# Basis products of a relational graph convolution: ten edge groups per product, one basis after each of eight groups

## The chip, the cores and the metric

The kernel runs on one core of a Trainium2 chip. The time is the device time of one execution in microseconds (us). The engines work in parallel, each through its own queue of instructions, and wait for each other through semaphores: TensorE (PE in the profile, with PEld for its weight loads) multiplies matrices into PSUM, VectorE (DVE) and ScalarE (ACT) work on tiles, GpSimd (POOL) here issues the indirect DMAs that gather rows, and SyncE (SP) issues most other DMAs.

## What is computed

A graph of 30,000 nodes with 128 features and 960,000 edges sorted by destination goes through two layers. The first holds two relational convolutions, whose 32 relation matrices are mixtures of 8 bases; the second holds a gated convolution with 4 edge types.

```python
def _rel_graph_conv(h, basis, coeff, bias, src, dst, etype, norm):
    W = jnp.einsum('rb,bdf->rdf', coeff, basis)          # R = 32, B = 8, D = 128
    Hr = jnp.einsum('nd,rdf->nrf', h, W)
    msg = Hr[src, etype] * norm
    agg = jax.ops.segment_sum(msg, dst, num_segments=N)
    return agg + bias
h = jax.nn.relu(_rel_graph_conv(feat, basis1, coeff1, bias1, src, dst, etype, norm))
out = _rel_graph_conv(h, basis2, coeff2, bias2, src, dst, etype, norm)
...
for t in range(T):                                       # the gated layer, T = 4
    eta = jax.nn.sigmoid(k[dst] + q[src])
    msg = jnp.where((edge_type == t)[:, None], eta * v[src], 0.0)
    agg = jax.ops.segment_sum(msg, dst, num_segments=n)
```

## The kernel before

There are three passes over the edges: pass 1 ("c1", first relational convolution), pass 2 ("c2", second) and pass 3 ("g", the gates). The change touches the body of passes 1 and 2, `rel_body` (from L415).

**Tiling.** 128 edges make one gather, G = 3 gathers a group, S = 5 groups a block (index `s`), NS = 20 blocks or NG = 100 groups one iteration of the device loop, and NI = 25 iterations a pass. So a pass has 7,500 gathers, 2,500 groups and 500 blocks. Every five blocks (SB) are a stage with loads of its own indices.

**A group.** GpSimd gathers the source nodes' rows of three times 128 edges into `hg` (L118; five buffers, so five groups or 15 gathers may be on their way). Since the edges are sorted, a group's destinations lie in a window of W = 32 nodes. VectorE builds for each gather a row block `sb` (L515, 12 buffers): for each of the 8 bases, the edge's coefficient where the window's column is the edge's destination. TensorE multiplies rows by `sb` and accumulates the three products of 128x256 into `pa` (L520, three buffers), which holds 8 bases x 32 columns. ScalarE copies `pa` into the block's tile `ab` (L524, two buffers).

**A block.** The bases are applied after the sum over edges. `bases_out(s - 1)` (L476 to L482) runs after group 1 of block `s`: eight products in a row, one per basis, each with the basis as weights and 5 x 32 = 160 columns of `ab[s - 1]`, accumulated in `po` (L479). After group 3 of block `s`, `add_windows` (L410 to L413) adds the five windows of `po[s - 2]` into the node sums `agg`, which lie in SBUF, at columns that come from registers; a stage's registers are loaded at L400, after group 3 of its second block.

**The rest of a block.** In pass 1 the coefficients are made on the way: `types` loads relation numbers (SyncE, L436), `onehot` after group 3 compares them (VectorE, `oh`, L444) and multiplies with the coefficients (TensorE, four products into `cp`, L449), `coefficients` after group 2 scales them (VectorE, `ce`, L459), and `keep` stores those of the second convolution. Pass 2 reads these back (`kept`). The constant `iw` that `sb` is compared with lies in the PSUM bank of `cp`. `beside(n)` runs the steps on finished nodes (`after_first`, `after_second`) that are due after group `n`.

**Order.** The engines' orders are as the code is written (`manual_schedule`); the tile framework adds the waits for data and for free buffers. At the end of an iteration the last block's products and the last two blocks' additions follow at once. `late` in an assertion (L338 to L340) is the first group by which all sums of earlier windows must be added, before the nodes' steps read them.

Of the kernel before, what the change touches and what calls it, by code (L numbers as in the profile page):

```python
# [19 lines left out]
P = 128  # L20
# [8 lines left out]
B = 8  # L29
# [5 lines left out]
W = 32  # L35
# [37 lines left out]
def kernel(  # L73
# [261 lines left out]
    def sorted_path():  # L335

        for u in range(NPI // VB):
            late = min(g for g in range(NG)  # L338
                       if min((g // S + 2) * S + S - 2, NG) > u * PERIOD + 1)
            assert (u + 1) * VB - late * NPI // NG <= LEAD  # L340
        with ExitStack() as all_:
            def edge_pass(name, body, after, banks, extra=None):
# [67 lines left out]
            def add_windows(po, base, s):  # L410
                for g in range(S):
                    to = agg[:, ds(base[s % SB * S + g], W)]
                    nc.vector.tensor_add(to, to, po[:, g, :])  # L413

            def rel_body(table, weights, second):  # L415
# [5 lines left out]
                def body(bas, i, io, pool, ps, cp, iw, ic, beside):  # L421
                    stage = {}
                    er, oh, pc, ce, ce_next, ab, po, base = {}, {}, {}, {}, {}, {}, {}, {}

                    def loads(k):
                        stage[k] = [stage_tile(io, "idx", src, I32, i, k),
                                    stage_tile(io, "relc", reld, F32, i, k),
                                    firsts(io, i, k)]
                        if not second:
                            stage[k].append(  # L430
                                stage_tile(io, "nrm", norm, F32, i, k, 4 * TQ - S * G))

                    def types(s):
                        er[s] = pool.tile([P, TQ, TP], I32, name="er")
                        for c in range(TQ):
                            nc.sync.dma_start(  # L436
                                er[s][:, c, :],
                                bass.AP(tensor=et32_row.tensor,
                                        offset=(i * NG + s * S) * GE + c * TP,
                                        ap=[[TQ * TP, 4], [0, R], [1, TP]]))  # L440

                    def onehot(s):
                        oh[s] = pool.tile([P, TQ, TP], F32, name="oh")
                        nc.vector.tensor_scalar(oh[s], er[s], icol4, None, op0=ALU.is_equal)  # L444
                        at = TQ * 8 * B
                        pc[s] = cp[:TP, at:2 * at].rearrange("p (c q l b) -> p c q l b", c=TQ, q=4,
                                                             l=2)
                        for c in range(TQ):
                            nc.tensor.matmul(pc[s][:, c].rearrange("p q l b -> p (q l b)"),  # L449
                                             lhsT=oh[s][:, c, :],  # L450
                                             rhs=coeff.rearrange("p q l b -> p (q l b)"),
                                             start=True, stop=True)

                    def coefficients(s):
                        t0 = s % SB * S * G
                        nrm = stage[s // SB][-1][:, t0:t0 + 4 * TQ]
                        for to, l in ((ce, 0), (ce_next, 1)):
                            to[s] = pool.tile([TP, 4, TQ, B], F32, name=f"ce{l}")
                            nc.vector.tensor_mul(  # L459
                                to[s], pc[s][:, :, :, l].rearrange("p c q b -> p q c b"),  # L460
                                nrm.rearrange("p (q c) -> p q c", q=4).unsqueeze(3).to_broadcast(
                                    [TP, 4, TQ, B]))
                            to[s] = to[s].rearrange("p q c b -> p (q c) b")

                    def block_rows(s):
                        return ce2[ds(i * NS + s, 1)].rearrange("o p e -> (o p) e")

                    def keep(s):
                        nc.scalar.dma_start(block_rows(s), ce_next[s][:, :S * G, :].rearrange(
                            "p t b -> p (t b)"))  # L470

                    def kept(s):
                        ce[s] = pool.tile([TP, S * G, B], F32, name="ce", bufs=4)
                        nc.sync.dma_start(ce[s].rearrange("p t b -> p (t b)"), block_rows(s))

                    def bases_out(s):  # L476
                        po[s] = ps.tile([P, S, W], F32, name="po")
                        for b in range(B):
                            nc.tensor.matmul(po[s].rearrange("p s w -> p (s w)"),  # L479
                                             lhsT=bas[:, b, :],  # L480
                                             rhs=ab[s][:, b].rearrange("p s w -> p (s w)"),
                                             start=(b == 0), stop=(b == B - 1))  # L482

                    loads(0)
                    if second:
                        kept(0)
                        kept(1)
                    else:
                        types(0)
                        onehot(0)  # L490
                        coefficients(0)
                        types(1)
                        onehot(1)
                    for s in range(NS):
                        k = s // SB
                        if s % SB == 0:
                            if s:
                                tc.stage_boundary()
                            if k + 1 < NQ:
                                loads(k + 1)  # L500
                        if s % SB == 2:
                            leave_stage()
                        idx, relc, start = stage[k][:3]
                        if s + 2 < NS:
                            (kept if second else types)(s + 2)
                        ab[s] = pool.tile([P, B, S, W], F32, name="ab")
                        for g in range(S):
                            t0 = (s % SB * S + g) * G
                            hg = pool.tile([TP, G, D], F32, name="hg", bufs=5)
                            for j in range(G):  # L510
                                gather(hg[:, j, :], table, idx[:, t0 + j:t0 + j + 1])
                            pa = ps.tile([P, B, W], F32, name="pa", bufs=3)
                            for j in range(G):
                                sb = pool.tile([TP, B, W], F32, name="sb", bufs=12)
                                nc.vector.scalar_tensor_tensor(  # L515
                                    sb, iw[:TP].unsqueeze(1).to_broadcast([TP, B, W]),
                                    relc[:, t0 + j:t0 + j + 1],
                                    ce[s][:, g * G + j, :].unsqueeze(2).to_broadcast([TP, B, W]),
                                    op0=ALU.is_equal, op1=ALU.mult)
                                nc.tensor.matmul(pa.rearrange("p b w -> p (b w)"),  # L520
                                                 lhsT=hg[:, j, :],
                                                 rhs=sb.rearrange("p b w -> p (b w)"),
                                                 start=(j == 0), stop=(j == G - 1))
                            nc.scalar.copy(ab[s][:, :, g, :], pa)  # L524
                            if g == 1 and s:
                                bases_out(s - 1)
                            if g == 2 and not second and s + 1 < NS:
                                coefficients(s + 1)
                            if g == 3 and not second:
                                keep(s)  # L530
                                if s + 2 < NS:
                                    onehot(s + 2)
                            if g == 3 and s > 1:
                                add_windows(po[s - 2], base[(s - 2) // SB], s - 2)
                            if g == 3 and s % SB == 1:
                                base[k] = bases(start, DVE)
                            beside(s * S + g)
                    bases_out(NS - 1)
                    for s in (NS - 2, NS - 1):
                        add_windows(po[s], base[NQ - 1], s)  # L540
                return start

            def gate_body(i, io, pool, ps, cp, iw, ic, beside):
# [497 lines left out]
```

## Time and profile before

| | |
|---|---|
| median of 10 runs | 33,956.33 us (33,933.54 to 33,987.04) |
| the profiled execution | 33,942.56 us |
| its span, first to last instruction | 33,940.8 us |
| mean granted TensorE clock | 0.677 of full |
| busy: TensorE / weight loads | 59% / 50% |
| busy: GpSimd / VectorE / ScalarE | 63% / 37% / 11% |
| pass 1, first to last gather | 170.2 to 11,499.2 us |
| pass 2 | 11,531.1 to 22,412.9 us |
| pass 3 | 22,455.4 to 33,910.1 us |

A row of the profile's groups names the source line, the engine, the operation, the tiles (out<-in) and their shape, then the count, the busy time, the mean duration of one in ns, and how long the engine stood idle just before these instructions with the releaser that ended most of it. An fp32 product shows as two records of matmul and two of weight load, so 8,000 basis products of both passes are 16,000 records. A gather (L118) is the time GpSimd takes to issue it; its data land later. "remote" names a semaphore that came late although its sender had long been done; "issue" is time in which nothing awaited shows. The chain that ended last is empty for this execution.

### The profile page before, as it was taken

Reading aid. Unit: us, or ns where it says so; the run is one execution under the profiler, and the core shown is the slowest. Engines: PE = TensorE matmul, PEld = TensorE weight load, DVE = VectorE, ACT = ScalarE, POOL = GpSimd, SP = SyncE. Lnnn points to the kernel's source line nnn. Section 1 sums busy time; section 2 is a strip of 40 time slices with the busy share of each in tenths; the row PEclk is TensorE's granted clock in tenths of the full one; section 3 lists DMA queues with packets and bytes.
Section 4 is the critical chain, followed back from the end, with each engine's and each line's share of the span. In section 5 each row is a group of like instructions: output and inputs, shape, how many; then the busy total and the mean of one; then the engine's idle time right before and its main releaser. Section 6 shows DMA issues by size and latency. Waiting matters only on the chain.

```text
span 33940.8 us, 321543 instructions
## 1 busy us (share of the span) xinstructions
PE 19859.2 (59%) x83304; PEld 16928.3 (50%) x83304; DVE 12397.5 (37%) x32695; ACT 3634.6 (11%) x9834; POOL 21338.8 (63%) x22514
## 2 busy tenths in 40 slices
PE   4555555555555565666666666655555555555555
PEld 3444444444444444444444444445555555555555
DVE  4333333333333333333333333333333333333333
ACT  1000000000000011111111111111111111111111
POOL 5666666666666666666666666666666666666665
PEclk7777777777777777777777777765555555555555
DMA  3222222222222222222222222234444444444444
GB/s 101 64 64 63 64 64 65 64 64 64 65 62 63 65 66 66 66 66 67 66 66 66 67 66 66 66 100 124 124 124 124 124 124 125 125 124 124 124 124 120
DMA packets 2171202, 2914.97 MB, mean 86 GB/s; under 512 B 684764, under 2 KB 1617880, under 8 KB 2169544
## 3 DMA queue, kind: packets, MB, share of 16 engines
q0 software_dynamic: 840000, 1967.52, 21.7%
q1 hardware_dynamic: 923347, 651.19, 6.6%
q10 hardware_dynamic: 406197, 276.11, 2.8%
q8 instruction: 802, 13.14, 0.2%
q14 instruction: 856, 7.01, 0.1%
HBM read 2618.79 MB, written 274.16 MB: 85 GB/s over the span
## 4 chain that ended last, share of the span: by engine, by line


## 5 line engine op out<-in xcount | busy, mean ns | idle before, releaser
L118 POOL DMA_INDIRECT hg<-h,idx x15000 | 14207.2, 947 | 8177.9 <-issue 4280.9
L520 PE MATMUL pa<-sb,hg 128*128 128x256 f32 x30000 | 9137.1, 462 | 5956.2 <-issue 3770.4
L520 PEld LDWEIGHTS pa<-sb,hg 128*128 128x128 f32 x30000 | 6848.7, 237 | 7745.1 <-issue 4196.6
L118 POOL DMA_INDIRECT qv<-qvtab,qi x7500 | 7104.6, 947 | 4392.7 <-issue 2261.3
L515 DVE SCALAR_TENSOR_TENSOR sb<-cp,relc,ce 128x256 f32<-128x256 f32 x15000 | 6133.9, 475 | 5281.9 <-remote 4211.6
L588 PE MATMUL po<-sel,msg 128*128 128x32 f32 x15000 | 3462.9, 387 | 4601.5 <-DVE msg L586 3925.0
L588 PEld LDWEIGHTS po<-sel,msg 128*128 128x128 f32 x15000 | 3426.7, 328 | 4889.3 <-DVE msg L586 4092.3
L577 PE MATMUL pk<-kw,oh 128*128 128x128 f32 x15000 | 3974.7, 438 | 140.8 <-issue 96.1
L618 DVE TENSOR_TENSOR pk<-pk,qv 128x384 f32<-128x384 f32 x2500 | 1406.4, 563 | 7099.9 <-remote 5179.8
L524 ACT COPY ab<-pa 128x256 f32<-128x256 f32 x5000 | 1813.0, 373 | 19833.4 <-remote 9555.0
L577 PEld LDWEIGHTS pk<-kw,oh 128*128 128x128 f32 x15000 | 3468.0, 331 | 143.5 <-issue 143.5
L479 PE MATMUL po<-ab,bas 128*128 128x160 f32 x16000 | 2525.0, 314 | 463.9 <-issue 268.7
L479 PEld LDWEIGHTS po<-ab,bas 128*128 128x128 f32 x16000 | 2435.1, 202 | 589.1 <-issue 315.4
L413 DVE TENSOR_TENSOR agg<-agg,po 128x32 f32 x7500 | 1399.2, 187 | 2697.8 <-ACT xs L692 684.5
L619 ACT ACTIVATE pk<-pk 128x384 f32<-128x384 f32 x2500 | 1187.5, 475 | 9412.2 <-DVE pk L618 6201.7
L715 PE MATMUL bank<-wall,hT 128*120 128x512 f32 x1524 | 1047.3, 811 | 1020.7 <-ACT hT L711 369.7
L586 DVE TENSOR_TENSOR msg<-pk,qv 128x384 f32<-128x384 f32 x2500 | 1363.9, 546 | 0.0
L449 PE MATMUL cp<-coeff,oh 128*128 128x64 f32 x4000 | 670.9, 307 | 770.0 <-issue 599.4
L449 PEld LDWEIGHTS cp<-coeff,oh 128*128 128x128 f32 x4000 | 668.6, 231 | 851.9 <-issue 748.0
L564 DVE TENSOR_TENSOR oh<-kb,cp 128x1920 f32<-128x1920 bf16 x500 | 1071.4, 2143 | 47.6 <-issue 31.8
L726 DVE TENSOR_TENSOR kt<-bank,ball 120x512 f32<-120x512 f32 x254 | 175.7, 692 | 2338.1 <-PE bank L715 1044.2
L715 PEld LDWEIGHTS bank<-wall,hT 128*120 128x120 f32 x1524 | 351.6, 248 | 1353.9 <-issue 627.4
(77 smaller groups left out, 3382.7 us busy)
## 6 DMA issues: line engine op xcount, KB each, us to landing
hg<-h,idx POOLq DMA_INDIRECT x15000
kb<-kcode SPq DMA_DIRECT2D x500, 480.0 KB
kw<-ktab SPq DMA_DIRECT2D x2500, 64.0 KB
er<-in_et_row SPq DMA_DIRECT2D x2000, 64.0 KB
qvtab<-qvt ACTq DMA_DIRECT2D x254, 480.0 KB
qv<-qvtab,qi POOLq DMA_INDIRECT x7500
ktab<-kt ACTq DMA_DIRECT2D x254, 240.0 KB
ce<-ce ACTq DMA_DIRECT2D x500, 60.0 KB
```

The lines of the kernel that those rows point to most:

```text
L118: nc.gpsimd.indirect_dma_start(out=to, out_offset=None, in_=table, in_offset=bass.IndirectOffsetOnAxis(ap=idx, axis=0))
L413: nc.vector.tensor_add(to, to, po[:, g, :])
L449: nc.tensor.matmul(pc[s][:, c].rearrange("p q l b -> p (q l b)"), lhsT=oh[s][:, c, :], rhs=coeff.rearrange("p q l b -> p (q l b)"), start= ...
L479: nc.tensor.matmul(po[s].rearrange("p s w -> p (s w)"), lhsT=bas[:, b, :], rhs=ab[s][:, b].rearrange("p s w -> p (s w)"), start=(b == 0), ...
L515: nc.vector.scalar_tensor_tensor(sb, iw[:TP].unsqueeze(1).to_broadcast([TP, B, W]), relc[:, t0 + j:t0 + j + 1], ce[s][:, g * G + j, :].uns ...
L520: nc.tensor.matmul(pa.rearrange("p b w -> p (b w)"), lhsT=hg[:, j, :], rhs=sb.rearrange("p b w -> p (b w)"), start=(j == 0), stop=(j == G ...
L524: nc.scalar.copy(ab[s][:, :, g, :], pa)
L577: nc.tensor.matmul(pk[n][:, j, :], lhsT=oh[n // S][:, n % S, j * TP:(j + 1) * TP], rhs=kw[n], start=True, stop=True)
L586: nc.vector.tensor_mul(msg, pk[n], qv[n][:, :, 1, :])
L588: nc.tensor.matmul(po[s][:, g, :], lhsT=msg[:, j, :], rhs=sel[s][:, g * G + j, :], start=(j == 0), stop=(j == G - 1))
L618: nc.vector.tensor_add(pk[n], pk[n], qv[n][:, :, 0, :])
L715: nc.tensor.matmul(bank(a, VB, T * D), lhsT=hT, rhs=wall[:, a].rearrange("p t f -> p (t f)"), start=True, stop=True)
```

## The change

Blocks are taken in pairs, `q = s // 2`, with ten groups. `ab` becomes one tile per pair of twice the size, and so does `po`. In place of eight products of 160 columns after group 1 of each block, one product of 320 columns follows each of the group positions 1 to 8 of the next pair: basis 0 after position 1, basis 7 after position 8. The ten windows of a pair are added together after position 9. At an iteration's end the last pair's eight products of 320 columns and its ten additions follow at once. The assertion's `late` is adapted to the later additions.

```diff
@@ -336,7 +336,7 @@
             late = min(g for g in range(NG)
-                       if min((g // S + 2) * S + S - 2, NG) > u * PERIOD + 1)
+                       if min(g // (2 * S) * 2 * S + 2 * S + B + 1, NG) > u * PERIOD + 1)
@@ -473,13 +473,18 @@
-                    def bases_out(s):
-                        po[s] = ps.tile([P, S, W], F32, name="po")
-                        for b in range(B):
-                            nc.tensor.matmul(po[s].rearrange("p s w -> p (s w)"),
-                                             lhsT=bas[:, b, :],
-                                             rhs=ab[s][:, b].rearrange("p s w -> p (s w)"),
-                                             start=(b == 0), stop=(b == B - 1))
+                    def basis_out(q, b):
+
+                        if b == 0:
+                            po[q] = ps.tile([P, 2 * S, W], F32, name="po")
+                        nc.tensor.matmul(po[q].rearrange("p s w -> p (s w)"),
+                                         lhsT=bas[:, b, :],
+                                         rhs=ab[q][:, b].rearrange("p s w -> p (s w)"),
+                                         start=(b == 0), stop=(b == B - 1))
+
+                    def add_pair(q):
+                        for s in (2 * q, 2 * q + 1):
+                            add_windows(po[q][:, s % 2 * S:(s % 2 + 1) * S, :], base[s // SB], s)
@@ -503,7 +508,9 @@
-                        ab[s] = pool.tile([P, B, S, W], F32, name="ab")
+                        q = s // 2
+                        if s % 2 == 0:
+                            ab[q] = pool.tile([P, B, 2 * S, W], F32, name="ab")
@@ -521,23 +528,23 @@
-                            nc.scalar.copy(ab[s][:, :, g, :], pa)
-                            if g == 1 and s:
-                                bases_out(s - 1)
+                            nc.scalar.copy(ab[q][:, :, s % 2 * S + g, :], pa)
+                            if q and 0 < s % 2 * S + g <= B:
+                                basis_out(q - 1, s % 2 * S + g - 1)
...
-                            if g == 3 and s > 1:
-                                add_windows(po[s - 2], base[(s - 2) // SB], s - 2)
+                            if q and s % 2 * S + g == B + 1:
+                                add_pair(q - 1)
...
-                    bases_out(NS - 1)
-                    for s in (NS - 2, NS - 1):
-                        add_windows(po[s], base[NQ - 1], s)
+                    for b in range(B):
+                        basis_out(NS // 2 - 1, b)
+                    add_pair(NS // 2 - 1)
                 return start
```

## The prediction

> **What bounds the kernel now.** I read the groups of instructions first, then the waits, the idle and busy stretches of each engine, and the timeline around two gaps. GpSimd is the busiest engine (63%), so its groups come first, with those that the change touches.
>
> ```profile
> L118 POOL DMA_INDIRECT hg<-h,idx x15000 | 14207.2, 947 | 8177.9 <-issue 4280.9
> L520 PE MATMUL pa<-sb,hg 128*128 128x256 f32 x30000 | 9137.1, 462 | 5956.2 <-issue 3770.4
> ...
> L524 ACT COPY ab<-pa 128x256 f32<-128x256 f32 x5000 | 1813.0, 373 | 19833.4 <-remote 9555.0
> ...
> L479 PE MATMUL po<-ab,bas 128*128 128x160 f32 x16000 | 2525.0, 314 | 463.9 <-issue 268.7
> ...
> L413 DVE TENSOR_TENSOR agg<-agg,po 128x32 f32 x7500 | 1399.2, 187 | 2697.8 <-ACT xs L692 684.5
> ```
>
> A gather takes 0.947 us, and where nothing is awaited the next follows 0.30 us later: a pace of 1.25 us. 7,500 gathers at 1.251 us are 9,383 us per pass. By the starts of the first and last gather the three passes took 11,329 us (pass 1, first relational layer), 10,882 (pass 2, second layer) and 11,455 (pass 3, gates). Counting every start in the trace, the excess over 1.25 us sits in single gaps: 720 in pass 1 (1,945 us, 2.70 each) and 636 in pass 2 (1,499 us, 2.36 each). These gaps are all that a change beside the gathers can move. The waits name who ends them:
>
> ```profile
> ACT ab L524 <- remote: 9555.0, 1105, 17.9
> ...
> DVE sb L515 <- remote: 4211.6, 524, 20.3
> ...
> POOL hg L118 <- remote: 2209.2, 898, 4.8
> ...
> POOL hg L118 <- PE pa L520: 1213.3, 606, 14.5
> ```
>
> (waiter, releaser: us in total, times, longest.) "remote" is a release by an engine that had been done long before. The timeline of two blocks in pass 1 shows it (start, duration, engine, count, idle time before):
>
> ```profile
> 8010.66 2.75 PE L520 MATMUL pa<-sb,hg 128*128 128x256 f32 x12
> 8013.25 1.00 PE L449 MATMUL cp<-coeff,oh 128*128 128x64 f32 x8
> ...
> 8020.11 0.95 POOL L118 DMA_INDIRECT hg<-h,idx  x1 [0.30 <-issue]
> ...
> 8024.17 0.37 ACT L524 COPY ab<-pa 128x256 f32<-128x256 f32 x1 [14.94 <-remote]
> ...
> 8024.47 4.79 DVE L515 SCALAR_TENSOR_TENSOR sb<-cp,relc,ce 128x256 f32<-128x256 f32 x12 [11.81 <-remote]
> 8024.64 0.95 POOL L118 DMA_INDIRECT hg<-h,idx  x1 [3.59 <-remote]
> ...
> 8031.43 2.34 PE L479 MATMUL po<-ab,bas 128*128 128x160 f32 x16
> ...
> 8042.41 0.94 POOL L118 DMA_INDIRECT hg<-h,idx  x1 [0.30 <-issue]
> ...
> 8046.84 0.37 ACT L524 COPY ab<-pa 128x256 f32<-128x256 f32 x1 [14.84 <-remote]
> ...
> 8047.07 0.94 POOL L118 DMA_INDIRECT hg<-h,idx  x1 [3.72 <-remote]
> ...
> 8047.54 1.08 DVE L413 TENSOR_TENSOR agg<-agg,po 128x32 f32 x5 [16.31 <-ACT ab L524]
> ```
>
> TensorE ended at 8014.25, yet the copy and the selection rows that need its signals start only at 8024.2. GpSimd, whose five group buffers (15 gathers) are then used up, stops, and all three resume within 0.5 us. Read one by one, the semaphore events show why: while gathers run, TensorE's increments and SyncE's issues come 0.70 us apart, as if one path took them in turn. Once the gathers have stopped and landed, those held back come 0.04 us apart. By the trace's counts a block of five groups has 28.0 increments of TensorE and 22.0 issues of SyncE in pass 1, so 0.70 x 50 = 35.0 us against a mean block of 11,329/500 = 22.66 us. In pass 2 it is 26.0 + 8.5 = 34.5, 24.2 us against 21.76. Both are over the block's time, so signals fall behind until a gap lets them out.
>
> TensorE isn't the bound: it is idle some 40% of both passes. One stretch in each of passes 1 and 2 (busy time of TensorE, its loads, VectorE, ScalarE and GpSimd, then the granted clock, DMA share and GB/s):
>
> ```profile
> 5000.00:6000.00 1000.00, 569.53 (x2461) 480.57 (x2459) 351.98 (x1050) 90.23 (x267) 635.16 (x671) 0.75 0.25 64
> 15000.00:16000.00 1000.00, 612.05 (x2344) 462.28 (x2344) 374.53 (x1080) 106.38 (x320) 652.97 (x691) 0.78 0.26 66
> ```
>
> **The change, part by part.** *Products.* A pair of blocks had 2 x 8 products of 160 columns and gets 8 of 320. The columns stay (2,560), so streaming costs 0. Half of the loads go (8,000 of 202 ns, which overlap the products). Hidden by TensorE's idle 40%; if that cover were gone, their exposed part would be a gain. Each product increments once, so a block has 4 increments fewer: 24.0 in pass 1, 22.0 in pass 2.
>
> *Pass 2, signals.* 0.70 x (22.0 + 8.5) = 21.35 us per block, just below the 21.76 that a block takes now. I take it that signals then set the pace: 500 x (21.35 - 21.76) = -205 us. Lower end: stalls shrink with the lag that a stall-free block gathers. Such a block is 15 x 1.251 = 18.77 us and takes 26.8 signals. The lag goes from (34.5-26.8)/34.5 = 0.22 to (30.5-26.8)/30.5 = 0.12, 46% less: -685 us. Upper end: the adds' new wait, below.
>
> *Pass 1, signals.* 0.70 x 46 = 32.2 us against 22.66: still far over. A gap lets everything out whether much or little is held, and costs about the same wherever it falls (784 us in 304 gaps before a block's third group, 233 in 105 before its second). So the time goes by the number of gaps. By the lag, (32.2-22.66)/(35.0-22.66) = 0.77, so 23% fewer: -440 us, the lower end. Upwards: eight increments in a row made one large lag per block, after which the next gap freed everything. One per group makes the lag small and steady, with no group free of it, and a gap that frees little is soon followed by another. Such repeats are there already: 84 of the 720 gaps follow the last one after only 3 gathers. One more gap per pair would be 250 x 2.70 = +675, the upper end. I take that the repeats double: 84 x 2.70 = +227 us. This is my weakest number.
>
> *Adds.* Still 7,500, 1.08 us per five. Ten now run at position 9 of a pair, one group behind the last product instead of some seven. In pass 1 VectorE's selection rows already wait, after position 8, for `cp` (their constant shares its bank), and TensorE runs `cp` behind that product: no new wait, 0. In pass 2 it is one. Behind the adds VectorE holds the next selection rows, for which TensorE waits, and GpSimd for its buffers. Twelve buffers of rows cover 4 groups, 4 x 3 x 1.251 = 15.0 us. The copies' waits of this kind last 9555/1105 = 8.6 us on average, so I take 0. If the cover is gone: a gap per pair, 250 x 2.36 = +590. Beside running gathers adds cost nothing: those of 8047.54 stand beside a gather of 0.95 us.
>
> *Edge of an iteration.* In pass 1 the last products, adds, `oh` and `cp` form a chain that GpSimd waits out (8.3 us before the sixth group of each iteration).
>
> ```profile
> 8309.64 2.52 PE L479 MATMUL po<-ab,bas 128*128 128x160 f32 x16 [0.46 <-issue]
> ...
> 8316.10 1.08 DVE L413 TENSOR_TENSOR agg<-agg,po 128x32 f32 x5 [11.35 <-remote]
> ```
>
> There five more adds stand in it (+1.08). The eight last products get twice as long: about 4.5 us at full clock, which their signals (8 x 0.70 = 5.6) cover, and about 9.1 at half clock, 3.5 more. Ends: 25 x 1.08 = +27 and 25 x 4.6 = +115. At a granted clock of 0.75, halfway, I take +71. Pass 2 has no such exposed chain, since GpSimd is ahead there.
>
> *Nothing else.* No DMA is added or moved past a queue; the products and adds issue none, and the register load (L400) stays where it is. Pass 3's code is untouched. `ab` and `po` are written again later than the product or add that frees them, behind work that is awaited anyway: 0.
>
> Sum: -205 + 227 + 71 = +93. The profiled execution took 33,942.6 us (span 33,940.8), 14 below the median of 33,956.3. So 34,036 for a run like it, and about 34,050 as a median.
>
> Two rules of the Trainium skill speak to this. "Advanced Engine Details and Errata", DMA Bandwidth Details, gives a semaphore increment on trn2 about 1 cycle. Here TensorE's come 0.70 us apart and up to 17.9 us late, so the row decides; by the page fewer increments would save nothing and the -205 would be 0. "TensorE: Matmul & The Clock Gate", Part 1, says that about 3.4 us of sustained work releases the full clock and an idle window takes it away, which speaks against spreading eight products. The trace agrees in kind: the clock was 1.00 for 10.24 us from 8006.05, then 0.50 for 13.65. If products alone lost the clock, the edge would be at +115 and the sum at +137.
>
> **Rivals.** (1) *Fewer signals, fewer gaps, in both passes; the other side.* For it: both passes are over the path's capacity, and most stalls (784 and 855 us) stand before the third group, whose buffer is freed right behind the eight products. Against it: the gap's cost doesn't go by what is held. Half of both lower ends, -220 - 343, with +71: -492, so about 33,460. It decides if gaps in pass 1 fall below 636 (720 less 227/2.70). (2) *No change:* the gaps move but keep their number and the edge is covered, about 33,960. For it: 7,500 gathers and five buffers remain. Against it: the signals per block fall by 8 and 12%, which should show. (3) *Adds stop VectorE in pass 2:* from a signal more than 15.0 us late at position 9. For it: waits up to 17.9 us. Against it: the mean of 8.6. +590 instead of -205: 34,845.
>
> **How the numbers follow.** Forecast (34,050; its own range 33,990 to 34,450) 0.43, rival 1 0.36, rival 2 0.10, rival 3 0.11. A measurement of this kernel can tell about 0.2% (68 us) from no change. So faster 0.36, same 0.10, slower 0.54. The range reaches a third beyond rival 1 (33,956 - 1.33 x 492 = 33,300) and, short of rival 3, to 34,650, which leaves out about 2 in 10.
>
> **What would show it.** Each step: 8,000 records of 128x320 in place of 16,000, with the same busy time; pass 2 near 10,680 us with fewer than 636 gaps; pass 1 near 11,630, with some 800 gaps and more runs of 3 gathers; iterations of pass 1 with a first long gap of about 11 us. I am wrong if pass 1 has fewer gaps (rival 1), if pass 2 gets longer with adds behind idle times over 15 us (rival 3), or if pass 3 moves.

## The result

The changed kernel took 34,558.19 us (median of 8, 34,441.97 to 34,601.69) against 33,957.99 (28 runs): a ratio of 1.0175, 95% interval 1.0166 to 1.0184. The profiled execution took 34,462.44 us, its span is 34,460.7; that is 520 us above the profiled execution of before, so the traces hold 520 of the medians' 600 us. Its groups and waits, to be set beside those of before:

```profile
L118 POOL DMA_INDIRECT hg<-h,idx x15000 | 14203.3, 947 | 8688.1 <-issue 4234.8
L527 PE MATMUL pa<-sb,hg 128*128 128x256 f32 x30000 | 9278.9, 458 | 6837.3 <-issue 5161.1
...
L531 ACT COPY ab<-pa 128x256 f32<-128x256 f32 x5000 | 1820.7, 373 | 20269.0 <-PE pa L527 9390.3
...
L480 PE MATMUL po<-ab,bas 128*128 128x320 f32 x8000 | 3071.6, 476 | 363.2 <-ACT ab L531 209.5
L413 DVE TENSOR_TENSOR agg<-agg,po 128x32 f32 x7500 | 1404.7, 187 | 2946.3 <-remote 1998.9
...
L480 PEld LDWEIGHTS po<-ab,bas 128*128 128x128 f32 x8000 | 1709.9, 215 | 744.1 <-ACT ab L531 228.6
```

```profile
ACT ab L531 <- remote: 8129.4, 1047, 17.9
...
DVE sb L522 <- remote: 5831.4, 541, 23.6
...
POOL hg L118 <- PE pa L527: 2039.5, 720, 16.7
...
POOL hg L118 <- remote: 1877.9, 820, 4.7
```

The products are halved in number as meant, their loads cost less (1,710 us for 2,435), and a gather still takes 947 ns. What grew is GpSimd's wait for products (`pa`), 1,213 to 2,040 us, and VectorE's wait with the selection rows, 4,212 to 5,831. GpSimd's waits on signals of an engine long done ("remote") fell.

Counting gaps between gathers as before (over 0.35 us beyond the pace of 1.25), with those of an iteration's first block, up to the start of its sixth group, apart:

| | before | changed |
|---|---|---|
| pass 1, first to last gather | 11,329 us | 11,841 us |
| gaps in first blocks | 279 us | 403 us |
| other gaps | 667, 1,637 us | 579, 2,032 us |
| how many of these before a block's third / fifth group | 294 / 148 | 48 / 309 |
| gaps over 5 us, first blocks included | 59, 413 us | 190, 1,369 us |
| pass 2, first to last gather | 10,882 us | 10,869 us |
| gaps in first blocks / others | 81 / 1,402 us | 203 / 1,270 us |
| pass 3 | 11,455 us | 11,467 us |

So all that was lost was lost in pass 1 (512 us): fewer gaps, but longer ones, and at another place in the block. A quarter of it, 124 us, lies in the first blocks. The timeline of the changed kernel shows one of the long gaps (start, duration, engine, count, idle time before):

```profile
8055.42 1.00 PE L449 MATMUL cp<-coeff,oh 128*128 128x64 f32 x8
...
8064.96 0.95 POOL L118 DMA_INDIRECT hg<-h,idx  x1 [0.30 <-issue]
8068.89 4.79 DVE L522 SCALAR_TENSOR_TENSOR sb<-cp,relc,ce 128x256 f32<-128x256 f32 x12 [16.31 <-remote]
...
8069.47 2.90 PE L527 MATMUL pa<-sb,hg 128*128 128x256 f32 x6 [13.05 <-issue]
...
8072.41 0.37 ACT L531 COPY ab<-pa 128x256 f32<-128x256 f32 x1 [13.06 <-PE pa L527]
8072.64 0.95 POOL L118 DMA_INDIRECT hg<-h,idx  x1 [6.74 <-PE pa L527]
```

The `cp` products ended at 8056.4. Their signal reached VectorE only after the gathers had stopped, at 8068.9. Until then no selection row could be built, since the constant they read lies in the bank of `cp`. TensorE therefore had nothing to multiply for 13 us. In the gaps shown of before, the products that free GpSimd's buffer had long run, and only their signal was missing: 3.6 us. Here rows and products still have to run inside the gap: 6.7. By that test (at least four records of `pa` and a selection row inside the gap) pass 1 had some 129 such gaps with 605 us and now has some 273 with 1,631 us; 25 of each, with 208 and 335 us, stand before an iteration's sixth group. Gaps without products inside fell from 549 (1,217 us) to 330 (737 us).

### The profile page after: what moved, and what is told of

Its sections match the earlier page's. It is cut to its first block, busy times and chain, and to the rows that moved or that the text cites. A ratio compares the mean times of both kernels' runs of the same rounds, so it can differ in the third digit from the quotient of the medians.

```text
span 34460.7 us, 305768 instructions
## 1 busy us (share of the span) xinstructions
PE 19691.9 (57%) x75304; PEld 16012.1 (46%) x75304; DVE 12425.2 (36%) x32695; ACT 3645.4 (11%) x9834; POOL 21335.6 (62%) x22514
## 4 chain that ended last, share of the span: by engine, by line
## 5 line engine op out<-in xcount | busy, mean ns | idle before, releaser
L527 PE MATMUL pa<-sb,hg 128*128 128x256 f32 x30000 | 9278.9, 458 | 6837.3 <-issue 5161.1
L527 PEld LDWEIGHTS pa<-sb,hg 128*128 128x128 f32 x30000 | 6750.8, 234 | 9044.2 <-issue 5977.9
L480 PE MATMUL po<-ab,bas 128*128 128x320 f32 x8000 | 3071.6, 476 | 363.2 <-ACT ab L531 209.5
L480 PEld LDWEIGHTS po<-ab,bas 128*128 128x128 f32 x8000 | 1709.9, 215 | 744.1 <-ACT ab L531 228.6
L449 PEld LDWEIGHTS cp<-coeff,oh 128*128 128x128 f32 x4000 | 586.0, 213 | 375.7 <-issue 282.9
L449 PE MATMUL cp<-coeff,oh 128*128 128x64 f32 x4000 | 567.1, 290 | 287.7 <-DVE oh L444 231.3
```

The lines of the kernel that those rows point to most:

```text
L480: nc.tensor.matmul(po[q].rearrange("p s w -> p (s w)"), lhsT=bas[:, b, :], rhs=ab[q][:, b].rearrange("p s w -> p (s w)"), start=(b == 0), ...
L527: nc.tensor.matmul(pa.rearrange("p b w -> p (b w)"), lhsT=hg[:, j, :], rhs=sb.rearrange("p b w -> p (b w)"), start=(j == 0), stop=(j == G ...
```

## The experiments

The ratios are to runs of the kernel before on the same chip, whose median stands beside them, since chips differ, as will be seen. The runs with 34,312 and 34,327 beside them are all of chip 9. The changed kernel itself was not run there; edge2, which differs from it only at the end of an iteration, is the nearest to it.

| run | us | before | ratio, 95% interval |
|---|---|---|---|
| a_irow | 34,744.79 | 34,312.46 | 1.0119 (1.0102 to 1.0136) |
| b_irow | 34,278.11 | 34,312.46 | 0.999 (0.998 to 0.9999) |
| row8 | 34,652.2 | 34,312.46 | 1.0094 (1.0077 to 1.0111) |
| spread16 | 34,637.01 | 34,312.46 | 1.0098 (1.0081 to 1.0115) |
| after2 | 28,510.13 | 28,477.55 | 1.0011 (1.0001 to 1.0021) |
| edge | 28,466.86 | 28,477.55 | 0.9997 (0.9987 to 1.0006) |
| a_ci | 28,488.49 | 28,477.55 | 1.0004 (0.9994 to 1.0014) |
| b_ci | 28,471.48 | 28,477.55 | 0.9997 (0.9987 to 1.0007) |
| a_ci2 | 28,424.78 | 28,417.94 | 1.0003 (0.9993 to 1.0012) |
| b_ci2 | 28,405.08 | 28,417.94 | 0.9995 (0.9986 to 1.0005) |
| edge2 | 34,767.17 | 34,327.06 | 1.0132 (1.0115 to 1.0149) |
| a_ci_edge | 34,121.16 | 34,327.06 | 0.994 (0.9922 to 0.9959) |

**1. Is it the wait for `cp`, or the spreading? (a_irow, b_irow)** In the changed kernel and in the one before, the rows read the constant from its SBUF tile.

```diff
-  sb, iw[:TP].unsqueeze(1).to_broadcast([TP, B, W]),
+  sb, irow[:TP].unsqueeze(1).to_broadcast([TP, B, W]),
```

> The changed kernel with the selection rows' constant read from its SBUF tile (irow) instead of the bank of cp, so that these rows no longer wait for cp's products. Theory L (lockstep: the long gaps of pass 1 are those in which VectorE, held by cp's late signal, and then TensorE still have work to do before a buffer comes free): gaps above 5 us in pass 1 fall from 190 to under 60, their sum from 2,435 to about 1,400 us, the time to 33,400-33,700. Theory S (products one at a time make TensorE slow or cold): the constant's place changes nothing there, 34,400-34,600.

> The kernel before with the same move of the constant. L: its 129 gaps of pass 1 that hold rows and products (605 us) become ordinary ones of 2.2 us, about -280 us, 33,600-33,750, and the changed kernel with this move is then no slower than this one. S: within 100 us of before, and the changed kernel stays 1.5% above it.

Theory L's times were missed by far, and b_irow came out as S has it, within 100 us of before. The traces say why. In a_irow the gaps with rows and products inside did fall, from 273 in the changed kernel (254 in edge2, on this chip) to 48, but the move slowed the gathers. One line of its instruction statistics (min/median/max in ns):

```profile
L118 POOL DMA_INDIRECT hg<-h,idx x15000: 938/944/7684, 169.8 to 23002.6; - x198
```

The median is unchanged, the longest is 7.7 us: 2,580 of the 15,000 gathers took over 1,000 ns (118 in the changed kernel), and what all of them took beyond 947 ns adds up to 1,278 us (25 in the changed kernel, 755 in b_irow). Against edge2, pass 1 of a_irow is 246 us shorter and pass 2, which has no `cp`, 249 us longer. So this pair shows that the long gaps vanish with the wait, but can't price it.

**2. Fewer signals, or products spread out? (row8, spread16)** The change does two things, so each is done alone: pairs with eight products in a row, and sixteen products of 160 columns, two after each position.

```diff
 row8
-  if q and 0 < s % 2 * S + g <= B:
-      basis_out(q - 1, s % 2 * S + g - 1)
+  if q and s % 2 * S + g == 1:
+      for b in range(B):
+          basis_out(q - 1, b)
 spread16
-      basis_out(q - 1, s % 2 * S + g - 1)
+      at = s % 2 * S + g - 1
+      two_out(2 * q - 2 + at // 4, at % 4)
...
```

`two_out(s, c)` multiplies bases 2c and 2c + 1 of block `s`, with a `po` for each block.

> Pairs as in the change, but the eight products of 320 columns in a row after position 1 (additions still after position 9). L: the signals are as few as in the changed kernel, so 34,350-34,700. S: the spreading is gone, so the time is back at 33,900-34,150.

> Pairs and spreading as in the change, but sixteen products of 160 columns, two after each of the positions 1 to 8, so that the signals are as many as before the change (28 and 26 per block). L: the time falls back to 33,850-34,150. S: it stays at 34,400 or more.

The expected times are those of the first chip. Taken as ratios to before, neither theory's numbers came: both runs land between, at 1.009 and 1.010. Either half of the change costs something, so "fewer signals" alone, L's first form, falls. Both runs also keep the pairs as such, and part of their cost lies in the first blocks, which experiment 4 takes up. The place of the gaps tells more (pass 1, outside first blocks, gaps before the third / the fifth group of a block; the traced execution of row8 is 120 us above its median):

| | third | fifth | all outside first blocks, us |
|---|---|---|---|
| before: eight in a row, 16 a pair | 294 | 148 | 1,637 |
| row8: eight in a row, 8 a pair | 231 | 204 | 1,803 |
| spread16: spread, 16 a pair | 104 | 256 | 1,948 |
| changed: spread, 8 a pair | 48 | 309 | 2,032 |
| edge2: as changed, but for an iteration's end | 62 | 281 | 2,051 |

The first and fourth rows are of another chip than the rest; edge2 shows that the changed order has nearly the same gaps on chip 9. Eight increments in a row stand just ahead of the products whose signal frees the third group's buffer, and the gap comes there. With fewer of them, or with them spread, fewer gaps fall there, and GpSimd more often runs on to the fifth group. Its buffer is freed by the fifth group's products of the block before, the first ones behind `cp`, whose rows must wait for `cp`'s signal. That is L's second form: not how many gaps, but where they fall. Experiment 4 tests it.

**3. The same wait taken away without touching SBUF, and the end of an iteration (after2, edge, a_ci, b_ci, then a_ci2, b_ci2).** In a_ci and b_ci (and their repeats) the constant of pass 1 gets a PSUM bank of its own; the two transposes of a node step share one bank to make room. `edge` leaves the constant where it is and treats an iteration's last pair as two halves, so that only eight products of 160 columns are left for the end.

```diff
 a_ci, b_ci
+  ci = cps.tile([P, 4 * D], F32, name="ci") if banks == 1 and extra else cp
-  iw, ic = cp[:, :W], cp[:, W:W + 1]
+  iw, ic = ci[:, :W], ci[:, W:W + 1]
...
-  got["pr"] = ps.tile([P, 4 * D], F32, name="bank")[:VB, :D]
-  got["px"] = ps.tile([P, 4 * D], F32, name="bank")[:, :VB]
+  both = ps.tile([P, 4 * D], F32, name="bank")
+  got["pr"], got["px"] = both[:VB, :D], both[:, D:D + VB]
...
-  edge_pass("c1", rel_body(h0, basis[0], False), after_first, 2, codes)
+  edge_pass("c1", rel_body(h0, basis[0], False), after_first, 1, codes)
 edge
+  if s == NS - 1 and g == 1:
+      half_out(NS // 2 - 1, 0)
...
-  for b in range(B):
-      basis_out(NS // 2 - 1, b)
+  half_out(NS // 2 - 1, S)
   add_pair(NS // 2 - 1)
```

> The changed kernel itself, on the chip of the next three. Both theories: 1.5 to 1.9% over the kernel before, with the extra gap time in pass 1 again.

> The changed kernel, but the last pair of an iteration as two halves of 160 columns: the first block's eight products after position 6, only the second block's eight at the end, as the kernel before has it. Theory E (the doubled end of an iteration costs what the gaps in the first block of an iteration grew by, 279 to 403 us in pass 1 and 81 to 203 in pass 2): these sums fall back to about 280 and 80, and the time by 200-300 us against the changed kernel. Rival: these gaps come from the spread products of the last pair but one, and the time moves by under 60 us.

> The changed kernel with the selection rows' constant in a PSUM bank of its own (in pass 1 the two transposes of a node step share one bank to make room), so that the rows don't wait for cp, and stay off SBUF. Theory L, refined (the change moves the gaps to the fifth group of a block, whose buffer is freed by products whose rows wait for cp): gathers keep 947 ns, gaps over 5 us outside the first blocks nearly vanish, pass 1's gap sum outside the first blocks falls from 2,032 to 1,400-1,650 us, the time by 350-600 us against the changed kernel. Rival S (the spread products themselves slow TensorE): under 100 us.

> The kernel before with the same bank for the constant. L: its 129 gaps with rows and products inside (605 us) become ordinary ones: 200-350 us less than before, gathers at 947 ns. S: within 100 us of before.

> The changed kernel with the constant's bank again, since on the chip of its first run no signal was late and no theory could show. If this chip's kernel before takes some 34,000 us: theory L (long gaps at the fifth group because rows wait for cp) expects 350-600 us less than the changed kernel's 1.75% above before, so a ratio to before of 0.998 to 1.007, with gaps over 5 us only at iterations' starts; rival S a ratio of 1.014 or more. If it takes some 28,500 us: 1.000 to 1.002 for both.

> The kernel before with the constant's bank, again. If signals are late on this chip: L 0.990 to 0.995 of before, S 0.998 to 1.002. If not: 1.000 for both.

These runs fell on two chips (13 and 10) on which the kernel before takes 28,478 and 28,418 us instead of 33,958, so the expected differences could not show: almost nothing is left to explain there. Waits and timeline of the changed kernel there (after2):

```profile
DVE sb L522 <- PE cp L449: 4090.1, 475, 16.2
...
PE pa L527 <- DMA hg<-h,idx: 3476.9, 4939, 3.3
```

```profile
8016.24 2.89 SPq L436 DMA_DIRECT2D er<-in_et_row  x4
...
8023.33 1.81 PE L449 MATMUL cp<-coeff,oh 128*128 128x64 f32 x8
...
8025.17 1.27 DVE L522 SCALAR_TENSOR_TENSOR sb<-cp,relc,ce 128x256 f32<-128x256 f32 x3 [8.96 <-PE cp L449]
...
8026.16 0.94 POOL L118 DMA_INDIRECT hg<-h,idx  x1 [0.30 <-issue]
```

The rows start 0.03 us after `cp` has ended, though gathers are running; no "remote" release stands among the large waits, and TensorE waits for the gathers' data, as it should. On one of TensorE's semaphores (number 110, which passes 1 and 2 both use), 0% of the increments come within 0.06 us of the one before, against 47 and 52% (passes 1 and 2) in the kernel before on the first chip and 32 and 37% in the changed one. SyncE's four issues (SPq) go out within 2.9 us. The gaps of all three passes together are 51 us in place of some 5,980. The same order of work, with signals in time, costs 0.1%. That is the strongest sign that the loss is made of late signals, though it is a comparison of chips, and no run says why these two let the signals through and others do not.

What the change costs there is the end of an iteration: 24 gaps of 1.86 us (45 us) in pass 1, one per iteration after the first, which `edge` brings down to 5 us in all; its time is 43 us lower. Theory E's mechanism holds there, at that small price. L can't show on these chips: a_ci and b_ci differ from before by no more than the measurement tells.

**4. Both on a chip with late signals (edge2, a_ci_edge).** The halved end, and the halved end with the constant's bank.

> The halved last pair again, in search of a chip with late signals. Where before takes some 34,000 us: theory E expects the first blocks' gap sums at about 280 (pass 1) and 80 us (pass 2) instead of 403 and 203, and a ratio to before of 1.009 to 1.012 (1.0175 less 200-300 us); its rival 1.016 or more. Where before takes some 28,400 us: 1.000 for E (the changed kernel had 24 gaps of 1.86 us there, 45 us), 1.001 for the rival.

> The changed kernel with both: the constant's own bank in pass 1 and the halved last pair. Where signals are late: L and E together leave the change without a cost, 0.985 to 1.000 of before; if it stays at 1.007 or more, a part of the cost has another cause. Where they are not: 0.999 to 1.000.

The two differ in the constant's bank, with the shared bank of the transposes that makes room for it, and by 646 us. Waits of edge2, then of a_ci_edge:

```profile
DVE sb L531 <- remote: 5607.2, 548, 23.7
...
POOL hg L118 <- PE pa L536: 2006.2, 752, 16.3
POOL hg L118 <- remote: 1967.6, 860, 3.9
```

```profile
POOL hg L118 <- remote: 2684.9, 984, 4.3
...
POOL hg L118 <- PE pa L537: 780.2, 439, 15.3
...
DVE sb L532 <- remote: 318.7, 173, 6.6
```

VectorE's late wait with the rows falls from 5,607 to 319 us, and GpSimd's wait for products from 2,006 to 780, while its wait for signals alone grows from 1,968 to 2,685. Pass 1 takes 11,259 us instead of 11,861; pass 2, which has no `cp`, 10,928 and 10,930. Gaps over 5 us in pass 1 go from 165 to 24, those with rows and products inside from 254 (1,505 us) to 49 (347, most of it before the sixth group of an iteration). The gaps still come before the fifth group (367 of 608 outside first blocks; 281 of 626 in edge2), but at 3.0 us each instead of 4.5. One of them in the timeline of a_ci_edge:

```profile
8018.44 2.90 PE L537 MATMUL pa<-sb,hg 128*128 128x256 f32 x6 [3.02 <-issue]
...
8024.40 0.94 POOL L118 DMA_INDIRECT hg<-h,idx  x1 [0.30 <-issue]
...
8028.54 0.65 ACT L541 COPY ab<-pa 128x256 f32<-128x256 f32 x2 [15.31 <-remote]
8028.78 0.94 POOL L118 DMA_INDIRECT hg<-h,idx  x1 [3.43 <-remote]
```

The products ran at 8018, before the gap, and the gap is only their signal: 3.4 us, like those of the kernel before. L, in its second form, holds: with the wait gone, nearly all gaps at that place cost a signal and no more. With both edits the change is faster than the kernel before (0.994).

E fails here: the first blocks have 421 and 183 us in edge2, near the changed kernel's 403 and 203 and not at 279 and 81; its ratio, 1.0132, lies between E's and the rival's. The growth, some 250 us in the two passes together, goes with the pairs. On this chip every kernel with pairs has it (row8, whose products are not spread, 448 and 354 us; spread16 383 and 207; a_ci_edge 359 and 181). With the constant in SBUF, a_irow has 414 and 302, and b_irow, without pairs, 280 and 95. So neither the doubled products of the end nor the spreading is needed for it. What in the pairs makes it stays open. Whether the kernel before gains from the constant's bank on such a chip wasn't seen; b_ci and b_ci2 ran only where no signal was late.

## Why the prediction was right, and where it was wrong

The sign was right, and the time (34,558) lies in the range and beyond the likeliest case's own (34,450): +600 us where +93 was added up. The sign was luck in part, since its largest term, pass 1, stood for more and shorter repeats, and there were fewer. By its steps:

- *What bounds the kernel:* right. Gathers kept 947 ns, the untouched pass 3 kept its time, and all that moved is gaps. On the chips with signals in time, the gaps are absent and the kernel before takes 5,500 us less.
- *Products:* half the records and loads, as said. The same busy time was not: 3,072 us for 2,525. No gap shows it, as TensorE is idle over 40%.
- *Pass 2, signals, -205:* 13 us were gained, with 645 gaps, not fewer than 636. Outside the first blocks it is -132, the right way; +122 in the first blocks, where nothing was expected, took it back. The term took 0.70 us a signal as a bound on the block, 21.35 us, but a block took 21.74; no run shows that bound. It also counted as SyncE's issues all that SyncE's queue runs: in pass 1 DMA issues are 5.5 of the 22.0 a block.
- *Pass 1, signals, +227:* the failing step. "A gap ... costs about the same wherever it falls", "so the time goes by the number of gaps", and short repeats double. The number fell (720 to 629, runs of 3 gathers from 84 to 66) and the mean gap rose from 2.7 to 3.9 us. A gap is cheap while only a signal is missing and dear when work is. Outside the first blocks this was +395 us; on chip 9 the constant's own bank takes these gaps from 2,051 to 1,519 us.
- *Adds:* "no new wait" for them in pass 1 fits: VectorE's late waits there stand at the rows (5,714 us, 432 at the additions). But the rows' wait for `cp` was used as cover and not priced itself. In pass 2 the additions' late waits grew from 232 to 1,567 us, yet rival 3's price of 590 us did not appear.
- *Edge, +71:* 45 us where signals are in time; +124 and +122 in passes 1 and 2 where they are late, of which the doubled end is not shown to be the cause. The gap before the sixth group of an iteration in pass 1 grew from 8.3 to 13.4 us on average, not to about 11.
- *Rival 1* was to decide at fewer than 636 gaps in pass 1. There were 629, and the time rose: the count was the wrong measure.

The rule on the clock, weighed there against spreading the products, didn't show: the granted clock of pass 1 stayed at 0.73 for 0.74 (2,000 to 9,000 us). Where signals are in time it is higher with the changed order, half as many products and spread, than with rows of eight, on one chip, a_ci2 first, then b_ci2 (the clock is the sixth value after the length):

```profile
2000.00:9000.00 7000.00, 4993.97 (x17458) 3143.34 (x17457) 3027.81 (x8804) 785.09 (x2229) 5283.51 (x5576) 0.90 0.30 77
```

```profile
2000.00:9000.00 7000.00, 5243.21 (x20486) 3736.83 (x20487) 3030.22 (x8819) 785.93 (x2234) 5294.59 (x5588) 0.84 0.30 77
```

## What to carry to other kernels

When a producer runs to the end of its buffers, ask of each place where it can stop what is still to be done there: only a signal, or work that itself waits. Removing a stall can move the stop to a dearer place, so price stalls by their place and not by their number. A constant that shares a PSUM bank with products made every reader here wait for them. Where signals were in time that cost next to nothing (1.0011 for after2, 1.0004 for a_ci); where they were late, 646 us.

## What was not expected of the hardware

- The same kernel took 33,958 us for the result, 34,312 on chip 9, and 28,478 and 28,418 on chips 13 and 10, at the same pace of gathers. What differs in the traces is TensorE's signals, held while gathers run (on one semaphore 47 to 52% come within 0.06 us of the one before) or not (0%).
- A row of VectorE that reads its constant from SBUF rather than PSUM left the median gather at 944 ns but made 2,580 of 15,000 longer than 1,000 ns, up to 7.7 us (a_irow; 2,538 in b_irow, 129 in row8 on the same chip).
- Half as many products, spread out, went with the higher granted clock where signals were in time, 0.90 for 0.84; where they were late it was 0.73 for 0.74.
